# Three elementwise additions of a two-layer graph attention kernel: on GpSimd, or inside accumulating DMAs

## Chip, cores and metric

One core of one Trainium2 chip runs the whole kernel. The metric is the device time of one execution in microseconds (us); less is better. Engines are named as in the profile: PE is TensorE's matmuls and PEld its weight loads, DVE is VectorE, ACT is ScalarE, POOL is GpSimd, SP is SyncE, which issues DMAs here.

## What is computed

The input x has 8 batches of 2048 rows of 256 floats, and one adjacency matrix of 2048 x 2048 serves both layers. All arithmetic is in fp32.

```
# layer 0: attention with 4 heads, a softmax of its own for each chunk of 256 keys
scores = clip(q @ k.T / 8, -10, 10), or -10 where adj == 0
ctx    = sum over the 8 chunks of softmax(scores) @ v
out    = ctx @ Wo.T + bo + x
out    = layernorm(out) * gamma + beta
x      = layernorm(x + out)
# layer 1: graph attention
Wh        = x @ W
e         = leaky_relu(s_i + s_j), -inf where there is no edge
h_prime   = softmax(e) @ Wh
x         = layernorm(x + elu(h_prime))
```

Three of these additions matter here: bo + x ahead of the first layer norm of layer 0, x + beta, which is added back after gamma, and x + elu(...) at the end of layer 1.

## The kernel before

Each batch is worked off in four blocks of 512 queries (`IB`), and each block in 8 chunks `j` of 256 keys, so that there are 8 x 4 x 8 = 256 steps `J`. A step has two halves, called beats; a beat takes about 8 us. The order of all instructions on every engine is written out by hand: a beat issues the scores of 128 keys, their exponentials, the products with v of the step before, and then lets every open generator advance by one `yield`. Each engine executes its own list in order, so an instruction that waits holds up all that stand behind it on its engine.

In layer 0, a beat has the score matmuls of both pairs of heads (L899), the clip and mask on VectorE (L909), the exponential on ScalarE (L912), and the products with v and with ones (L928). The sum of a chunk's weights travels by small DMAs (`dc`, `rd`, `r`, L944 to L956) and comes back as a factor; VectorE multiplies the chunk's product with it (L963, into `un`), and GpSimd adds it to the running context `ctxT` (L964).

Layer 1 of a batch runs beside layer 0 of the next one, at most 1.5 steps of 128 neighbours a beat. A step is a sum on ScalarE (L714), leaky relu (L718) and edge mask (L723) on VectorE, an exponential (L727) on ScalarE, four matmuls (L746, in the last batch L761), and for the row sums an addition on GpSimd into `acc` (L734, L736). Maxima over the edges are made ahead on VectorE (L438), from rows `fb` that DMAs bring. When layer 0 of the last batch is over, layer 1 of the last two batches' blocks remains as a tail.

Two generators hold the changed lines.

- `fin(b, ib, ctxT)` ends a block of layer 0. It is opened three chunks before the block's end. It loads 512 rows of x (L346, by SP), and one beat later GpSimd makes y = x + bo (L349) and x = x + beta (L350), both on 128 x 1024 floats. Once the context is ready, the output projection runs on TensorE (L357), VectorE adds it to y (L364), statistics follow (`stats`, L316 to L322), ScalarE normalizes (L329), GpSimd multiplies with gamma and adds x (L370, L371; in the very last block VectorE does this), and a second layer norm gives the rows of layer 1, which are stored to HBM (`h_d`, L376) and transposed by TensorE (L383).
- `fin1(b, ib, hx, acc)` ends a block of layer 1 in all batches but the last. It loads the block's input rows from `h_d` into `hr` (L591), forms row sums on TensorE (L597), divides on ScalarE (L601), takes the exponential (L603), makes elu on VectorE (L605), has GpSimd add `hr` (L606), and then comes a layer norm and the store (L611). The last batch has a function of its own, `fin1_last`, which adds on VectorE (L632) and is not changed.

The tiles `x`, `y`, `hx` and `hr` have one buffer each: a block's first write to one of them waits until the block before has done with it. The helper `bc_rows(v)` views a row of 256 floats, which lies in all 128 partitions, as four equal rows, so that it fits 128 x 4 x 256.

Of the kernel before, what the change touches and what calls it, by code (L numbers as in the profile page):

```python
# [9 lines left out]
F32 = mybir.dt.float32  # L10
# [4 lines left out]
ALU = mybir.AluOpType  # L15
# [4 lines left out]
P = 128  # L20
# [8 lines left out]
def tile_adj_attention__then__gat(  # L29
# [35 lines left out]
    nc = tc.nc  # L65
    B, N, F = x.shape
# [4 lines left out]
    IB = 512  # L71
    NIB = N // IB
    TPB = IB // P
# [13 lines left out]
    one = ctx.enter_context(tc.tile_pool(name="one", bufs=1))  # L87
# [130 lines left out]
    def row_bc(name, v):  # L218
        t = const.tile([P, F], F32, name=name)
        nc.sync.dma_start(out=t, in_=v.partition_broadcast(P))  # L220
        return t

    bo_bc = row_bc("bo_bc", bo)
    gamma_bc = row_bc("gamma_bc", gamma)
    beta_bc = row_bc("beta_bc", beta)
# [3 lines left out]
    for n in range(2):  # L229
        t = one.tile([P, F], F32, tag=("hx", "ex")[n], name=f"a_bc{n}")  # L230
# [80 lines left out]
    def stats(src, name):  # L311

        st = two.tile([P, TPB, 6], F32, tag="st", name=f"st_{name}")
        mv = two.tile([P, TPB, 2], F32, tag="mv", name=f"mv_{name}")
        for t in range(TPB):
            nc.vector.bn_stats(st[:, t, :], src[:, t, :])  # L316
            nc.vector.bn_aggr(mv[:, t, :], st[:, t, :])
            if t == TPB // 2 - 1 and beat < 2 * NIB * NCH:
                yield
        rstd = two.tile([P, TPB], F32, tag="rstd", name=f"rstd_{name}")  # L320
        nc.vector.tensor_scalar_add(rstd, mv[:, :, 1], EPS)
        nc.gpsimd.tensor_tensor(rstd, rstd, nhalf, ALU.pow)  # L322
        return mv, rstd

    def normalize(dst, mv, rstd, name):
        nmr = two.tile([P, TPB], F32, tag="nmr", name=f"nmr_{name}")
        nc.vector.scalar_tensor_tensor(nmr, mv[:, :, 0], -1.0, rstd, ALU.mult, ALU.mult)
        for t in range(TPB):
            nc.scalar.activation(  # L329
                dst[:, t, :], dst[:, t, :], AF.Identity, bias=nmr[:, t : t + 1], scale=rstd[:, t : t + 1]  # L330
            )

    def bc_rows(v):
        return v.unsqueeze(1).to_broadcast([P, TPB, F])

    h_d = dram.tile([B, NIB, P, TPB, F], F32, name="h_d")
# [5 lines left out]
    def fin(b, ib, ctxT):  # L342


        xt = one.tile([P, TPB, F], F32, tag="x", name=f"x{b}_{ib}")
        nc.sync.dma_start(out=xt, in_=x[b, ts(ib, IB), :].rearrange("(t p) f -> p t f", p=P))  # L346
        yield
        y = one.tile([P, TPB, F], F32, tag="y", name=f"y{b}_{ib}")
        nc.gpsimd.tensor_add(y, xt, bc_rows(bo_bc))  # L349
        nc.gpsimd.tensor_add(xt, xt, bc_rows(beta_bc))  # L350
        while (b, ib) not in ctx_done or ctx_done[b, ib] == beat:
            yield
        for t2 in range(TPB // 2):
            po = ps_m.tile([P, 2, F], F32, tag="m", name=f"po{b}_{ib}_{t2}")
            for j in range(2):
                for k in range(KC):
                    nc.tensor.matmul(  # L357
                        po[:, j, :],
                        ctxT[:, k, ts(2 * t2 + j, P)],
                        WT["o"][:, k, :],  # L360
                        start=(k == 0),
                        stop=(k == KC - 1),
                    )
            nc.vector.tensor_add(y[:, ts(t2, 2), :], po, y[:, ts(t2, 2), :])  # L364
        mv, rstd = yield from stats(y, f"a{b}_{ib}")
        yield
        normalize(y, mv, rstd, f"a{b}_{ib}")
        yield
        engine = nc.vector if (b, ib) == (B - 1, NIB - 1) else nc.gpsimd
        engine.tensor_mul(y, y, bc_rows(gamma_bc))  # L370
        engine.tensor_add(y, y, xt)  # L371
        yield
        mv, rstd = yield from stats(y, f"b{b}_{ib}")
        yield
        normalize(y, mv, rstd, f"b{b}_{ib}")
        nc.sync.dma_start(out=h_d[b, ib], in_=y)  # L376
        fin_near[b] += 1
        yield
        hT = four.tile([P, KC, IB], F32, tag="xT", name=f"hT{b}_{ib}")
        for k in range(KC):  # L380
            pt = ps_m.tile([P, TPB, P], F32, tag="m", name=f"pt{b}_{ib}_{k}")
            for t in range(TPB):
                nc.tensor.transpose(pt[:, t, :], y[:, t, ts(k, P)], ident)  # L383
            nc.scalar.copy(hT[:, k, :], pt.rearrange("p t c -> p (t c)"))
        if (b, ib) == (B - 1, NIB - 1):
            states[b]["hT"] = hT
        else:
            nc.sync.dma_start(out=hT_d[b, ib], in_=hT)
# [198 lines left out]

    def fin1(b, ib, hx, acc):

        hr = one.tile([P, TPB, F], F32, tag="hr", name=f"hr{b}_{ib}")  # L590
        nc.sync.dma_start(out=hr, in_=h_d[b, ib])  # L591
        yield


        pr = ps_m.tile([P, TPB], F32, tag="m", name=f"pr{b}_{ib}")
        for t in range(TPB):
            nc.tensor.matmul(pr[:, t : t + 1], acc[:, ts(t, P)], ones[:, 0:1], start=True, stop=True)  # L597
        r = two.tile([P, TPB], F32, tag="r1", name=f"r1{b}_{ib}")
        nc.vector.reciprocal(r, pr)
        for t in range(TPB):  # L600
            nc.scalar.activation(hx[:, t, :], hx[:, t, :], AF.Identity, bias=ones[:, 0:1], scale=r[:, t : t + 1])  # L601
        ex = one.tile([P, TPB, F], F32, tag="ex", name=f"ex{b}_{ib}")
        nc.scalar.activation(ex, hx, AF.Exp, bias=shifts[:, 1:2])  # L603
        yield
        nc.vector.scalar_tensor_tensor(hx, ex, 1.0, hx, ALU.min, ALU.max)  # L605
        nc.gpsimd.tensor_add(hx, hx, hr)  # L606
        yield
        mv, rstd = yield from stats(hx, f"c{b}_{ib}")
        yield
        normalize(hx, mv, rstd, f"c{b}_{ib}")  # L610
        nc.sync.dma_start(out=out[b, ts(ib, IB), :].rearrange("(t p) f -> p t f", p=P), in_=hx)  # L611
# [92 lines left out]
    class Step:  # L704
# [33 lines left out]
        def product(self):  # L738
# [29 lines left out]
            if last:  # L768
                blocks_done += 1
                tag = "y" if k["b"] == B - 1 and k["ib"] % 2 else "hx"  # L770
                hx = one.tile([P, TPB, F], F32, tag=tag, name=f"hx{self.name}")
                if k["b"] < B - 1:
                    nc.scalar.copy(hx, k["us"])
                else:
                    r = two.tile([P, TPB], F32, tag="r1", name=f"r1{self.name}")
                    for n in range(TPB // 2):
                        nc.vector.reciprocal(r[:, ts(n, 2)], k["us"][n][:, :, F])

                    for t in (0, 2):
                        nc.scalar.activation(  # L780
                            hx[:, t, :],
                            k["us"][t // 2][:, t % 2, 0:F],
                            AF.Identity,
                            bias=ones[:, 0:1],
                            scale=r[:, t : t + 1],
                        )
                        nc.vector.tensor_scalar(
                            hx[:, t + 1, :],
                            k["us"][t // 2][:, t % 2 + 1, 0:F],
                            r[:, t + 1 : t + 2],  # L790
                            1.0,
                            ALU.mult,
                            ALU.add,
                        )
                    fins.append(fin1_last(k["b"], k["ib"], hx))
                    return
                fins.append(fin1(k["b"], k["ib"], hx, k["acc"]))
# [75 lines left out]
    for J in range(total + 1):  # L873
        b, ib, j = J // (NIB * NCH), J // NCH % NIB, J % NCH
# [4 lines left out]
        for half in range(2):  # L879
# [37 lines left out]
            if prev is not None:  # L917
                if half == 0:

                    pool, tag = (one, "hr") if early and J % 3 == 2 else (two, "un")  # L920
                    prev["un"] = pool.tile([P, 2, IB], F32, tag=tag, name=f"un{prev['name']}")
                for part in ((2, 0), (1,))[half]:
# [14 lines left out]
                    else:  # L937
# [7 lines left out]
                            out=dc, in_=ds.rearrange("(h m) (n w) -> h m n w", m=DH, n=DH)[:, 0, :, :]  # L945
# [12 lines left out]
                        def scaled(p=prev):  # L958
                            r2 = p["r"].unsqueeze(1).to_broadcast([P, 2, IB])
                            if p["j"] == 0:  # L960
                                nc.vector.tensor_mul(p["ctxT"], p["un"], r2)
                            else:
                                nc.vector.tensor_mul(p["un"], p["un"], r2)  # L963
                                nc.gpsimd.tensor_add(p["ctxT"], p["ctxT"], p["un"])  # L964
                            if p["j"] == NCH - 1:
                                ctx_done[p["b"], p["ib"]] = beat
                            if p["j"] == NCH - 3:
                                fins.append(fin(p["b"], p["ib"], p["ctxT"]))
# [66 lines left out]
```

## Time and profile before

| | |
|---|---|
| runs | 4401.98, 4400.04, 4389.66 us; median 4400.04 |
| the profiled execution | 4387.29 us, its span 4385.5 us |
| busy in the span | PE 4064.2, DVE 3417.7, ACT 2564.4, POOL 1760.5 us |
| mean granted TensorE clock | 0.98 |
| DMA engines, mean busy share | 30.5% of 16 engines' span, 415.63 MB moved |
| L349, L350, L606 on POOL | 32, 32 and 28 instructions, 2426, 2693 and 2853 ns on average |

A group of instructions is shown as line, engine, operation, what it writes and reads by the program's names, partitions x elements, and how often; then its busy time and the mean duration of one in ns; then the idle time of its engine just before it and what ended most of that idle time. Durations come from the one profiled execution. DMA issues on SP are in the trace as instructions of SP's queue (SPq); they are not counted as busy, and what they move shows only as DMA time.

### The profile page before, as it was taken

The page shows a single profiled execution, that of the slowest core. Times are in us where ns is not written, and L with a number is a line of the kernel's source. Part 1 is how long each engine was busy: PE and PEld are TensorE (multiplying, and loading weights), DVE is VectorE, ACT ScalarE, POOL GpSimd, SP SyncE. Part 2 cuts the span into 40 slices and gives each one's busy share as a digit, 9 for nine tenths or more (in the row PEclk, how much of TensorE's full clock was granted, in tenths as well). Part 3 has the DMA queues.
Part 4 walks back from the last instruction along what each step waited for, and adds up shares of the span by engine and source line. Part 5 has one row for each costly group of instructions (what it writes and reads, how often), then busy time and mean ns, then how long its engine had stood idle before and what let it go on. Part 6 is the DMA issues. An engine that isn't in the chain of part 4 may idle for free. (4 is left out here: it accounts for less than half of the span.)

```text
span 4385.5 us, 61171 instructions
## 1 busy us (share of the span) xinstructions
PE 4064.2 (93%) x23053; PEld 1907.6 (43%) x23053; DVE 3417.7 (78%) x4530; ACT 2564.4 (58%) x3842; POOL 1760.5 (40%) x901
## 2 busy tenths in 40 slices
PE   8889989999999999999899999999999999899767
PEld 3223334454344534454344543445434454344456
DVE  5876589965998669976699766996579965888777
ACT  5655556665566556666566665566556665555546
POOL 0222235543455334444245442554325542354420
PEclk9999999999999999999999999999999999999889
DMA  5554232222332233321333223232232222322321
GB/s 166 182 163 149 71 115 86 83 73 89 99 90 81 64 107 102 100 75 51 105 102 98 74 74 105 85 95 78 70 106 85 89 78 67 115 83 80 123 73 58
DMA packets 257641, 415.63 MB, mean 95 GB/s; under 512 B 85440, under 2 KB 120512, under 8 KB 256448
## 3 DMA queue, kind: packets, MB, share of 16 engines
q1 hardware_dynamic: 257344, 411.71, 30.5%
q8 instruction: 181, 2.97, 0.3%
q14 instruction: 116, 0.95, 0.1%
HBM read 340.66 MB, written 68.88 MB: 93 GB/s over the span
## 5 line engine op out<-in xcount | busy, mean ns | idle before, releaser
L912 ACT ACTIVATE e<-sc 128x1024 f32<-128x1024 f32 x1024 | 1034.2, 1020 | 1049.9 <-DVE sc L909 1006.7
L909 DVE SCALAR_TENSOR_TENSOR sc<-sc,mk 128x1024 f32<-128x1024 f32 x1024 | 1206.7, 1223 | 538.3 <-PE sc L899 352.6
L899 PE MATMUL sc<-qT,kT 64*128 64x512 f32 x4096 | 1060.4, 633 | 86.7 <-ACT e L912 86.2
L964 POOL TENSOR_TENSOR ctxT<-ctxT,un 128x1024 f32<-128x1024 f32 x224 | 568.5, 2538 | 1145.3 <-DVE un L963 1007.0
L928 PE MATMUL u<-e,v 128*32 128x512 f32 x8192 | 980.9, 597 | 0.0
L746 PE MATMUL us<-wh,w 128*128 128x256 f32 x3584 | 878.6, 395 | 81.9 <-ACT w L727 60.4
L746 PEld LDWEIGHTS us<-wh,w 128*128 128x128 f32 x3584 | 667.7, 193 | 422.2 <-ACT w L727 110.7
L736 POOL TENSOR_TENSOR acc<-acc,w 128x512 f32<-128x512 f32 x392 | 601.7, 1535 | 544.9 <-ACT w L727 534.4
L899 PEld LDWEIGHTS sc<-qT,kT 64*128 64x128 f32 x4096 | 347.2, 189 | 611.6 <-ACT e L912 281.8
L718 DVE SCALAR_TENSOR_TENSOR w<-ab,sj,w 128x512 f32<-128x512 f32 x512 | 571.5, 1137 | 4.6 <-ACT w L714 4.5
L928 PEld LDWEIGHTS u<-e,v 128*32 128x32 f32 x8192 | 240.6, 110 | 659.7 <-issue 543.9
L928 PE MATMUL u<-e,ones 128*32 128x512 f32 x4096 | 497.5, 604 | 0.0
L723 DVE TENSOR_TENSOR w<-w,mk 128x512 f32<-128x512 f32 x512 | 458.6, 917 | 37.1 <-DMA mk<-mask 34.6
L438 DVE CUSTOM_DVE_ANT_0 fb<-sj_row,fb 128x1024 bf16<-128x1024 f32 x240 | 387.8, 1626 | 2.3 <-DMA fb<-far 2.3
L714 ACT ACTIVATE w<-ab,sj 128x512 f32<-128x512 f32 x512 | 352.2, 714 | 8.7 <-POOL acc L734 5.4
L727 ACT ACTIVATE w<-w 128x512 f32<-128x512 f32 x512 | 308.8, 629 | 75.9 <-DVE w L723 75.3
L936 ACT COPY un<-u 128x512 f32<-128x512 f32 x512 | 300.5, 587 | 66.5 <-PE u L928 57.6
L963 DVE TENSOR_TENSOR un<-un,r 128x1024 f32<-128x1024 f32 x224 | 278.1, 1242 | 42.2 <-DMA r<-rd 36.7
L928 PEld LDWEIGHTS u<-e,ones 128*32 128x32 f32 x4096 | 107.8, 110 | 356.5 <-issue 305.4
L950 DVE RECIPROCAL dc<-dc 128x16 f32<-128x16 f32 x256 | 63.9, 249 | 149.8 <-DMA dc<-ds 134.0
L942 ACT COPY ds<-u 128x512 f32<-128x512 f32 x256 | 148.5, 580 | 3.0 <-PE u L928 2.5
L349 POOL TENSOR_TENSOR y<-x,bo_bc 128x1024 f32<-128x1024 f32 x32 | 77.6, 2426 | 163.6 <-DMA x<-in_x_dram 103.0
(112 smaller groups left out, 3114.7 us busy)
## 6 DMA issues: line engine op xcount, KB each, us to landing
r<-rd SPq DMA_DIRECT2D x256, 256.0 KB
mk<-mask SPq DMA_DIRECT2D x120, 512.0 KB
fb<-far SPq DMA_DIRECT2D x240, 256.0 KB
xT_k<-in_xT_dram SPq DMA_DIRECT2D x32, 512.0 KB
raw<-in_adjT_dram SPq DMA_DIRECT2D x32, 512.0 KB
rawf<-in_adj_dram SPq DMA_DIRECT2D x32, 512.0 KB
x<-in_x_dram SPq DMA_DIRECT2D x32, 512.0 KB
h_d<-y SPq DMA_DIRECT2D x32, 512.0 KB
```

Source lines behind the costliest of these rows:

```text
L438: nc.vector.tensor_tensor_reduce(out=fb, in0=row, in1=fb, scale=1.0, scalar=2 * FAR * 0.999, op0=ALU.add, op1=ALU.max, accum_out=dst,)
L714: nc.scalar.activation(self.w, k["ab"][:, 1, :], AF.Identity, bias=k["sj"][:, 1, c : c + 1])
L718: nc.vector.scalar_tensor_tensor(self.w, k["ab"][:, 0, :], k["sj"][:, 0, c : c + 1], self.w, ALU.add, ALU.max)
L723: nc.vector.tensor_tensor(self.w, self.w, self.k["mks"][self.c // HT][:, self.c % HT, :], ALU.min)
L727: nc.scalar.activation(self.w, self.w, AF.Exp)
L736: nc.gpsimd.tensor_add(k["acc"], k["acc"], self.w)
L746: nc.tensor.matmul(k["us"][:, t, :], self.w[:, ts(t, P)], k["wh"][c // TPB][:, c % TPB, 0:F], start=(first and t % 2 == 0), stop=last, ski ...
L899: nc.tensor.matmul(sc[:, h, :], kTs[b][c // TPB][h * D : (h + 1) * D, hp, ts(c % TPB, P)], qT[h * D : (h + 1) * D, hp, :], start=True, sto ...
L909: nc.vector.scalar_tensor_tensor(scs[hp], scs[hp], -CLIP, cap, ALU.max, ALU.min)
L912: nc.scalar.activation(e, scs[hp], AF.Exp)
L928: nc.tensor.matmul(m[h * DH : (h + 1) * DH, :], prev["v"][pc // TPB][:, pc % TPB, f0 : f0 + DH] if part < 2 else ones[:, 0:DH], prev["es"] ...
L964: nc.gpsimd.tensor_add(p["ctxT"], p["ctxT"], p["un"])
```

## The change

In `fin`, the tile x is first filled with rows of beta and the tile y with rows of bo, by DMAs from SBUF to SBUF that SP issues. Then two DMAs that GpSimd issues bring the rows of x from HBM and add them to what lies in the tile, first to x and, one beat later, to y. In `fin1`, the tile `hr` and its load go; a DMA that GpSimd issues brings the rows of `h_d` and adds them onto elu's result, and the statistics come one beat later than before.

```diff
     def fin(b, ib, ctxT):
         xt = one.tile([P, TPB, F], F32, tag="x", name=f"x{b}_{ib}")
-        nc.sync.dma_start(out=xt, in_=x[b, ts(ib, IB), :].rearrange("(t p) f -> p t f", p=P))
+        nc.sync.dma_start(out=xt, in_=bc_rows(beta_bc))
         yield
         y = one.tile([P, TPB, F], F32, tag="y", name=f"y{b}_{ib}")
-        nc.gpsimd.tensor_add(y, xt, bc_rows(bo_bc))
-        nc.gpsimd.tensor_add(xt, xt, bc_rows(beta_bc))
+        nc.sync.dma_start(out=y, in_=bc_rows(bo_bc))
+        x_rows = x[b, ts(ib, IB), :].rearrange("(t p) f -> p t f", p=P)
+        nc.gpsimd.dma_start(out=xt, in_=x_rows, accum_op=ALU.add)
+        yield
+        nc.gpsimd.dma_start(out=y, in_=x_rows, accum_op=ALU.add)
         while (b, ib) not in ctx_done or ctx_done[b, ib] == beat:
             yield
...
     def fin1(b, ib, hx, acc):
-        hr = one.tile([P, TPB, F], F32, tag="hr", name=f"hr{b}_{ib}")
-        nc.sync.dma_start(out=hr, in_=h_d[b, ib])
         yield
...
         nc.vector.scalar_tensor_tensor(hx, ex, 1.0, hx, ALU.min, ALU.max)
-        nc.gpsimd.tensor_add(hx, hx, hr)
+        nc.gpsimd.dma_start(out=hx, in_=h_d[b, ib], accum_op=ALU.add)
+        yield
         yield
         mv, rstd = yield from stats(hx, f"c{b}_{ib}")
```

On GpSimd's list 92 DMA issues stand where 92 additions stood; SP's list has 64 issues where it had 60. The wait for beta's rows lies on GpSimd, ahead of the first accumulating DMA, and the wait for the y of the block before lies on SP, ahead of the load of bo's rows. In the changed kernel the two accumulating DMAs of `fin` are lines 352 and 354, which the prediction names so.

## The prediction

> **What bounds the kernel now.** I read the page's busy shares first, then the waits of TensorE, then the groups of GpSimd and VectorE, then the timeline where the changed lines run.
>
> ```profile
> PE 4064.2 (93%) x23053; PEld 1907.6 (43%) x23053; DVE 3417.7 (78%) x4530; ACT 2564.4 (58%) x3842; POOL 1760.5 (40%) x901
> ```
>
> TensorE is the bound: its 4064 us stay as they are. No change off TensorE can be worth more than its idle time, 4385.5 - 4064.2 = 321 us. Its waits (us in total, times, longest):
>
> ```profile
> PE sc L899 <- ACT e L912: 86.2, 57, 6.3
> PE us L746 <- ACT w L727: 60.4, 43, 10.8
> ...
> PE po L357 <- POOL ctxT L964: 16.4, 13, 2.6
> ```
>
> The first two end chains that pass through VectorE (L909 feeds e, L723 feeds w). GpSimd ends only 16.4 us of TensorE's waits, so unloading GpSimd by itself is worth little. The stages (length, then busy us of PE, PEld, DVE, ACT, POOL; granted clock) show one exception to TensorE's rule:
>
> ```profile
> 660.00:3950.00 3290.00, 3125.59 (x17920) 1471.19 (x17912) 2602.62 (x3393) 1959.91 (x2962) 1454.82 (x749) 0.99 0.29 87
> 4110.00:4245.00 135.00, 78.53 (x314) 55.85 (x310) 114.66 (x176) 50.53 (x90) 58.38 (x29) 0.78 0.34 109
> ```
>
> From 4110 to 4245 us VectorE is 85% busy and TensorE 58%: there VectorE sets the pace. Now the three GpSimd groups that go (busy, mean ns):
>
> ```profile
> L350 POOL TENSOR_TENSOR x<-x,beta_bc 128x1024 f32<-128x1024 f32 x32 | 86.2, 2693 | 2.5
> L606 POOL TENSOR_TENSOR hx<-hx,hr 128x1024 f32<-128x1024 f32 x28 | 79.9, 2853 | 43.2 <-DVE hx L605 43.2
> ...
> L349 POOL TENSOR_TENSOR y<-x,bo_bc 128x1024 f32<-128x1024 f32 x32 | 77.6, 2426 | 163.6 <-DMA x<-in_x_dram 103.0 <-PE sc L899 50.4 <-PE pv L275 10.2
> ```
>
> VectorE's two-input operations have long tails (min/median/max ns):
>
> ```profile
> L718 DVE SCALAR_TENSOR_TENSOR w<-ab,sj,w x512: 651/746/2884, 620.5 to 4366.9; 128x512 f32<-128x512 f32 x171
> L723 DVE TENSOR_TENSOR w<-w,mk x512: 674/685/2862, 628.4 to 4367.7; 128x512 f32<-128x512 f32 x171
> ```
>
> The timeline says why. Two L723, 1.4 us by their median, took 4.85 us while L349 and L350 ran:
>
> ```profile
> 2015.15 2.38 POOL L349 TENSOR_TENSOR y<-x,bo_bc 128x1024 f32<-128x1024 f32 x1
> 2017.61 2.69 POOL L350 TENSOR_TENSOR x<-x,beta_bc 128x1024 f32<-128x1024 f32 x1
> ```
>
> ```profile
> 2015.99 4.85 DVE L723 TENSOR_TENSOR w<-w,mk 128x512 f32<-128x512 f32 x2
> ```
>
> **What the Trainium skill says.** (1) "SBUF — State Buffer", section "Who interferes with whom": a VectorE instruction with two SBUF inputs shares a read port with a GpSimd instruction that reads SBUF, and one waits for the other to finish. The trace agrees: 4.85 us against 1.4. (2) "DMA: Bandwidth & Descriptors", "SWDGE vs HWDGE vs iDMA": an accumulating DMA is GpSimd's alone, and its cores write the descriptors; nothing before shows it. (3) Same page, "Anatomy of one DMA — SWDGE (gpsimd) path": about 2.0 us + bytes/436 GB/s, descriptor building "small, variable". (4) "Collectives: The Full Stack", "The bandwidth ceiling": the add costs two source reads in place of one.
>
> **The change, part by part.**
>
> *Removed from GpSimd:* 77.6 + 86.2 + 79.9 = 243.7 us of 1760.5. Off the path, as shown.
>
> *Removed from VectorE: stalls.* Each group's mean on the page, above its fastest instruction: L718 512 x (1137-651) = 249 us, L723 512 x (917-674) = 124, L438 240 x (1626-1186) = 106, small rows some 70; in all about 550. By share of busy GpSimd the removed lines own 244/1760 = 14%, 76 us. By the timeline, giving each instruction's excess to the GpSimd operations that it overlaps, it is L349 25, L350 70, L606 34: 129 us. I take 129; 76 is the low end.
>
> *How much reaches the end.* In 660 to 3950, TensorE idles 0.10 us per 2 us on average. Summed over the 24 pairs L349/L350 there, it idles 23.3 us in the stretch 6 to 16 us after L349 starts, where the average gives 12; over 25 L606, 10.9 us at 4 to 8 us after, where it gives 5. The excess is 17 us; part belongs to other work at that place, so I take 12 (0 to 17). In the tail VectorE leads: L718 at 4124.9 took 2.83 us, L723 at 4127.8 2.71, L438 at 4138.9 3.37, L718 at 4233.8 2.83; above their usual 0.75, 0.69, 1.21, 0.75 that is 8.3 us. At 4131.86 the chain waits for a transfer of fb anyway, so I take 6 (3 to 8). Five pairs before 660: 2 (0 to 4). Sum: 20 us, from 3 to 29.
>
> *Added on SP:* beta rows take the place of x (32 for 32), 32 bo rows come, 28 hr go: 4 issues more x 0.47 us (x's median) = 2 us, at nothing, since SP mostly waits. Behind y's bo rows stand L952 and L956 (rd, r), whose user L963 comes two beats later (a beat is about 8 us). y's rows wait on SP for the previous y's transposes, done 30 us or more earlier in every block: no new wait. If that cover went, SP would hold up every r.
>
> *Added on GpSimd:* 92 DMA issues. The trace has none; the nearest row is SP's 0.47 us, the upper end the whole fixed-plus-transfer time, 2.0 + 0.52 MB/436 GB/s = 3.2 us, doubled for two reads' sake to 6.6. I take 2.0 us: 184 us, so GpSimd gains 60. L352 waits for beta's rows as L349 waited for x (103.0 us, 12 times), with the same size and place on SP; behind it stand L964 and L736.
>
> *Landing.* Time from issue to use: I take 2.0 + 4.4 (two reads: 2.0 + 2 x 1.2) = 6.4 us, from 3.2 to 13. The cover is one extra beat in each place. The tightest are (b,0), where x landed at 1618.5 and L364 wants y at 1636.5 (18 us for 2.0 + L964's 2.4 + 6.4 = 10.8), and (b,3) of layer 1, where L605 ends at 1023.8 and the statistics, one beat later than now, come at about 1034: 10 us for 6.4. Everywhere else it is 16 us or more. So nothing is late at my value. On VectorE's and ScalarE's queues nothing else moves than these statistics and their scaling, one beat back, behind that beat's L909, L963, L718 and L723; TensorE's queue keeps its order. The store of hx slips the same beat, 8 us, of the 41 us or more before the next L773. The DMA engines are 29% busy in the long stage, so the extra 0.5 MB a block finds room.
>
> *Sum.* Against the profiled execution (4387.3, span 4385.5): 4387.3 - 20 = 4367. The median of the runs shown is 12.7 higher: 4400 - 20 = **4380**.
>
> **The rivals.** *A, the forecast:* 4380, own range 4360 to 4387. *B, the stall only moves:* L964 and L736 start earlier and block VectorE instead, or descriptor building holds the same port. For it: L736 and L964 already own 338 of the 550 us. Against: 2.4 us adds back to back are the longest block there is. About 5 us left: 4395. *C, the stall costs more:* if VectorE's lateness also triggers the half-speed stretches of TensorE's clock, 40% of 129 us shows: 4350. *D, the rows land late (slower):* building and landing at 6.6 us each. Then (b,0) needs 13.2 + 2.4 + 6.6 = 22.2 us of 18: 4.2 x 8 = 34 us of VectorE waiting at L364; (b,3) 13.2 of 10.2: 3 x 7 = 21; GpSimd gains 92 x 6.6 - 244 = 363 us of work, which doubles L357's wait for ctxT: 16; the last L606 in the tail, 5. 76 - 20 = +56: 4456. It decides from building plus landing of about 10 us. For it: VectorE is in order, so one late row holds everything. Against: x's plain load takes under 7 us even behind 1 MB of sj_row (1611.9 to 1618.5).
>
> **How the numbers follow.** A 0.55, B 0.18, C 0.07, D 0.20. About 0.3% (13 us) is what a measurement can tell from no change. Faster: A and C, 0.62; within: B, 0.18; slower: D, 0.20. The range must leave out no more than 0.2: from C's 4348 to part of D, 4440.
>
> **What would show it.** Right: L718, L723, L438 means down by 10 to 25%, VectorE busy some 100 us less, L364 and the statistics L316 not waiting for x or h_d rows, TensorE's busy time unchanged. Wrong: VectorE idle until DMA y or hx; GpSimd blocked by its own issues with L357 waiting more for L964; or VectorE means unchanged, with the excess on L736 and L964.

## The result, and the profile after

The changed kernel takes 4444.65 us (median of 5 runs, 4440.60 to 4445.86) against 4399.86 us (5 runs) before: a ratio of 1.0108, with a 95% interval of 1.0098 to 1.0119. It is slower by 45 us, where 20 us of gain were forecast. The profiled execution took 4443.71 us, its span 4441.9 us, 56.4 us more than before's.

The page of the changed kernel, its busy shares and the two large DMA queues (packets, MB, share of 16 engines' span; "software" is GpSimd's queue):

```profile
PE 4082.2 (92%) x23053; PEld 1915.9 (43%) x23053; DVE 3273.9 (74%) x4530; ACT 2568.0 (58%) x3842; POOL 1576.0 (35%) x901
...
q1 hardware_dynamic: 270208, 413.81, 30.3%
q0 software_dynamic: 37824, 48.24, 7.0%
```

Both engines that were to be relieved were: VectorE is busy 144 us less, GpSimd 185. TensorE's idle time grew all the same, from 321 to 360 us, so something else makes it wait. The other 18 of the 56 us are busy time: TensorE's matmuls took 4082.2 us in place of 4064.2, and its mean granted clock was 0.973 in place of 0.980. VectorE's operations did become shorter at their means (L718's 1137 ns to 1107, L723's 917 to 765, L438's 1626 to 1515); the medians had little to lose:

```profile
L721 DVE SCALAR_TENSOR_TENSOR w<-ab,sj,w x512: 651/746/2859, 638.1 to 4423.0; 128x512 f32<-128x512 f32 x171
L726 DVE TENSOR_TENSOR w<-w,mk x512: 673/683/2849, 645.9 to 4423.8; 128x512 f32<-128x512 f32 x171
```

GpSimd's three groups of DMA issues in the place of the additions:

```profile
L352 POOL DMA_DIRECT2D x<-in_x_dram x32 | 43.6, 1363 | 176.8 <-DMA x<-beta_bc 111.9 <-DVE dc L953 47.9 <-DVE sc L912 17.0
L354 POOL DMA_DIRECT2D y<-in_x_dram x32 | 46.1, 1442 | 47.2 <-DMA y<-bo_bc 25.4 <-PE u L931 19.2 <-issue 2.5
L608 POOL DMA_DIRECT2D hx<-h_d x28 | 25.4, 908 | 43.3 <-DVE hx L607 38.5 <-ACT w L730 2.1 <-ACT w L717 1.9
```

They cost 115 us. From issue to landing the medians are 6.3 us (L352), 7.0 (L354) and 5.7 (L608), the longest 13.4; in the first block of batches 1 to 7, L354's took 12.1 to 12.8. Now TensorE's waits after:

```profile
PE sc L902 <- ACT e L915: 79.1, 56, 6.4
PE us L749 <- ACT w L730: 67.8, 45, 8.2
PE po L361 <- POOL ctxT L967: 56.2, 8, 8.5
PE pab L465 <- ACT ds L945: 25.6, 12, 3.2
```

The third line is the find: the output projection waited 16.4 us in 13 waits, the longest 2.6; now it is 56.2 in 8, one in each batch. The name at the end, GpSimd's addition into `ctxT`, is only the last link. VectorE's waits, before and then after, tell what came ahead of it:

```profile
DVE dc L950 <- DMA dc<-ds: 134.0, 98, 4.7
...
DVE fb L438 <- DMA fb<-far: 2.3, 4, 1.0
```

```profile
DVE dc L953 <- DMA dc<-ds: 214.9, 119, 7.6
...
DVE fb L442 <- DMA fb<-far: 51.9, 16, 7.3
...
DVE y L368 <- DMA y<-in_x_dram: 7.8, 1, 7.8
```

Before, VectorE waited for rows `fb` 2.3 us in all; now 51.9. Both lines that grew wait for transfers that the change doesn't touch. For the rows that the accumulating DMAs bring to `y` it waits once, in the last block of the first batch.

The timeline of one place, where the first block of a batch ends, shows the whole chain (start, duration, engine, instruction; in brackets the idle time before it and what ended it):

```profile
1637.76 0.33 SPq L425 DMA_DIRECT2D sj_row<-sj_d  x1
1638.14 0.90 SPq L434 DMA_DIRECT2D fb<-far  x2
1639.14 0.64 SPq L347 DMA_DIRECT2D x<-beta_bc  x1
...
1644.31 0.63 SPq L350 DMA_DIRECT2D y<-bo_bc  x1
...
1646.89 1.35 POOL L352 DMA_DIRECT2D x<-in_x_dram  x1 [15.67 <-DVE dc L953]
...
1649.75 0.92 SPq L140 DMA_DIRECT2D mk<-mask  x1
...
1650.04 1.84 POOL L354 DMA_DIRECT2D y<-in_x_dram  x1
...
1651.75 1.47 SPq L434 DMA_DIRECT2D fb<-far  x2
...
1660.99 1.23 DVE L442 CUSTOM_DVE_ANT_0 fb<-sj_row,fb 128x1024 bf16<-128x1024 f32 x1 [5.84 <-DMA fb<-far]
...
1663.63 1.22 DVE L966 TENSOR_TENSOR un<-un,r 128x1024 f32<-128x1024 f32 x1
...
1665.00 2.33 POOL L967 TENSOR_TENSOR ctxT<-ctxT,un 128x1024 f32<-128x1024 f32 x1 [13.13 <-DVE dc L953]
...
1667.39 2.08 PE L361 MATMUL po<-WT_o,ctxT 128*128 128x256 f32 x4 [8.15 <-POOL ctxT L967]
```

Read it from the bottom. TensorE waited 8.15 us for `ctxT`; GpSimd made it as soon as VectorE's L966 had run; L966 stood on VectorE's list behind L442, which waited 5.84 us for the `fb` rows issued at 1651.75, 9 us before. The line of L361 shows the first four of the projection's 16 matmuls. The same place before:

```profile
1628.35 1.23 DVE L438 CUSTOM_DVE_ANT_0 fb<-sj_row,fb 128x1024 bf16<-128x1024 f32 x1 [0.64 <-DMA fb<-far]
...
1630.65 0.08 DVE L438 DVE_READ_ACCUMULATOR2_ANT m<- 128x1 f32 x1
1630.65 1.22 DVE L963 TENSOR_TENSOR un<-un,r 128x1024 f32<-128x1024 f32 x1
...
1634.41 3.72 PE L357 MATMUL po<-WT_o,ctxT 128*128 128x256 f32 x16 [2.60 <-POOL ctxT L964]
```

The wait costs more than its own length. All 16 matmuls of the projection took 6.45 us after, where they took 3.72 before. The stretch of the projection, before and then after (length, busy us of PE, PEld, DVE, ACT, POOL, granted clock, DMA share, GB/s):

```profile
1634.40:1642.00 7.60, 7.59 (x44) 4.33 (x48) 6.47 (x16) 1.42 (x2) 0.73 (x1) 1.00 0.34 105
```

```profile
1667.40:1675.00 7.60, 7.60 (x22) 5.59 (x24) 3.96 (x8) 1.40 (x2) 0.00 (x0) 0.64 0.34 105
```

The granted clock was 0.64 there in place of 1.00. Batches 1 to 7 all show it: ahead of the first block's projection TensorE waited 0.3 to 2.6 us before and 6.5 to 8.5 after, and the projection took 5.3 to 6.5 us after, against 3.72 before in six of the seven. In sum that is 46 us more of waiting and 13 more of projection.

And why the rows came late. The stretch around those loads, in the same columns, first before, then after:

```profile
1611.00:1619.00 8.00, 8.00 (x54) 2.40 (x56) 3.99 (x5) 3.80 (x5) 0.36 (x1) 1.00 0.75 265
...
1622.00:1630.00 8.00, 7.12 (x50) 1.97 (x52) 7.36 (x9) 3.55 (x6) 5.64 (x2) 1.00 0.57 159
```

```profile
1638.00:1647.00 9.00, 9.00 (x62) 2.66 (x64) 3.97 (x5) 3.80 (x5) 0.11 (x1) 1.00 0.93 285
...
1649.00:1659.00 10.00, 9.70 (x64) 2.56 (x64) 6.15 (x7) 4.51 (x6) 2.88 (x2) 1.00 0.99 216
```

Where the `fb` rows are due, the DMA engines were 57% busy, and are 99% busy now for 10 us. The mean over the long stage, 0.29 before and 0.36 after, shows none of this.

To place the loss, the start of each score matmul (L899, L902) after is set against its start before, in the two profiles. How much each kind of stretch grew (us; one profile each, so that some us are chance):

| stretch | growth |
|---|---|
| batches 1 to 7, first block | -7.1 |
| second block: its first beats, where `fin` of the first block runs | +50.2 (5.1 to 10.0 in each batch) |
| third block | -15.7 |
| fourth block (beats 4 to 6) | +19.3 |
| first batch, with the start | +10.2 |
| tail | -0.5 |

### The profile page after: what moved, and what is told of

The parts are those of the page before. It is cut to its first block, busy times and chain, and to the rows that moved or that the text cites. A ratio compares the mean times of both kernels' runs of the same rounds, so it can differ in the third digit from the quotient of the medians.

```text
span 4441.9 us, 61341 instructions
## 1 busy us (share of the span) xinstructions
PE 4082.2 (92%) x23053; PEld 1915.9 (43%) x23053; DVE 3273.9 (74%) x4530; ACT 2568.0 (58%) x3842; POOL 1576.0 (35%) x901
## 5 line engine op out<-in xcount | busy, mean ns | idle before, releaser
L915 ACT ACTIVATE e<-sc 128x1024 f32<-128x1024 f32 x1024 | 1037.2, 1021 | 1146.6 <-DVE sc L912 1099.9
L912 DVE SCALAR_TENSOR_TENSOR sc<-sc,mk 128x1024 f32<-128x1024 f32 x1024 | 1206.2, 1223 | 549.9 <-PE sc L902 308.7
L902 PE MATMUL sc<-qT,kT 64*128 64x512 f32 x4096 | 1054.9, 629 | 79.7 <-ACT e L915 79.1
L967 POOL TENSOR_TENSOR ctxT<-ctxT,un 128x1024 f32<-128x1024 f32 x224 | 555.7, 2481 | 1251.9 <-DVE un L966 1019.5
L739 POOL TENSOR_TENSOR acc<-acc,w 128x512 f32<-128x512 f32 x392 | 584.9, 1492 | 585.8 <-ACT w L730 575.7
L902 PEld LDWEIGHTS sc<-qT,kT 64*128 64x128 f32 x4096 | 344.7, 188 | 604.1 <-ACT e L915 268.7
L721 DVE SCALAR_TENSOR_TENSOR w<-ab,sj,w 128x512 f32<-128x512 f32 x512 | 556.0, 1107 | 17.3 <-ACT w L717 17.1
L726 DVE TENSOR_TENSOR w<-w,mk 128x512 f32<-128x512 f32 x512 | 380.9, 765 | 38.1 <-DMA mk<-mask 35.5
L442 DVE CUSTOM_DVE_ANT_0 fb<-sj_row,fb 128x1024 bf16<-128x1024 f32 x240 | 361.7, 1515 | 51.9 <-DMA fb<-far 51.9
L966 DVE TENSOR_TENSOR un<-un,r 128x1024 f32<-128x1024 f32 x224 | 272.6, 1217 | 38.0 <-DMA r<-rd 37.8
L361 PE MATMUL po<-WT_o,ctxT 128*128 128x256 f32 x512 | 133.9, 418 | 60.4 <-POOL ctxT L967 56.2
```

Of the source, the lines that this page charges most:

```text
L442: nc.vector.tensor_tensor_reduce(out=fb, in0=row, in1=fb, scale=1.0, scalar=2 * FAR * 0.999, op0=ALU.add, op1=ALU.max, accum_out=dst,)
L721: nc.vector.scalar_tensor_tensor(self.w, k["ab"][:, 0, :], k["sj"][:, 0, c : c + 1], self.w, ALU.add, ALU.max)
L726: nc.vector.tensor_tensor(self.w, self.w, self.k["mks"][self.c // HT][:, self.c % HT, :], ALU.min)
L739: nc.gpsimd.tensor_add(k["acc"], k["acc"], self.w)
L902: nc.tensor.matmul(sc[:, h, :], kTs[b][c // TPB][h * D : (h + 1) * D, hp, ts(c % TPB, P)], qT[h * D : (h + 1) * D, hp, :], start=True, sto ...
L912: nc.vector.scalar_tensor_tensor(scs[hp], scs[hp], -CLIP, cap, ALU.max, ALU.min)
```

## The experiments

The theory after these views, *crowding*: where a batch begins, the two fills and the two accumulating DMAs of `fin` fill the DMA engines just when the `fb` rows are due; VectorE's list waits, then `ctxT`, then TensorE. Rivals: the statistics that `fin1` moves one beat back cost the time; GpSimd's list is held at L354 by the wait for bo's rows; or the fills' place in SyncE's queue, ahead of the `fb` loads, and not the engines' time. The expectations name theories by numbers as they stood when each was written. "Second block" and "fourth block" below are the growth of those rows of the table.

**1. Only the change of `fin1`.** The diff of `fin1` as in the change; `fin` as before.

> Only the part in fin1 is changed: h + elu by an accumulating DMA, statistics one beat later; fin adds on GpSimd as before. Theory 1 (crowded DMA engines in the first block of each batch delay fb's rows and hold VectorE's list, and the moved statistics collide with layer 0's in the fourth block): the collision costs about 20 us, the L606 stalls that are gone give back about 8, so about 4412 us, between 4400 and 4422, with the steps at (b,3) of about 4 us and none at the end of (b,0). Theory 2 (GpSimd's list stands at L354, which waits for bo's rows, ahead of the last addition to ctxT): nothing of the loss is here, about 4390. Theory 3 (accumulated rows land late): VectorE waits at the statistics, some 2 us x 28, about 4450.

Measured: 4387.79 us, 0.9982 (0.9975 to 0.9988). This half is a small gain, against the expectation. Second block +3.4, third -14.8, fourth +24.7: the loss in the fourth block belongs here, the one in the second doesn't.

**2. Only the change of `fin`.** The diff of `fin` as in the change; `fin1` as before.

> Only the part in fin is changed: bo and beta rows filled by SP, x accumulated onto both; fin1 adds hr on GpSimd as before, statistics where they were. Theory 1: the 7 to 8 us at the end of every (b,0) stay, the 4 us in (b,3) go: about 4430 us, between 4420 and 4440. Theory 2: all of the loss is here: about 4445. Theory 3: about 4420, with L368 waiting for y.

Measured: 4449.28, 1.0124 (1.0110 to 1.0137). Second block +46.5, first batch with the start +11.9, third -0.5, fourth -2.0. So the loss is all `fin`'s, nearly all of it at one place of batches 1 to 7, and taking L349 and L350 off GpSimd gained nothing anywhere else. The halves add up: +54 us here and -8 in experiment 1 make 46; the whole change measured 45.

**3. Before, with the second `yield` of `fin1` alone.**

```diff
         nc.gpsimd.tensor_add(hx, hx, hr)
         yield
+        yield
         mv, rstd = yield from stats(hx, f"c{b}_{ib}")
```

> The kernel before with nothing but the second yield behind GpSimd's addition in fin1, so that the statistics of layer 1 come one beat later; no DMA accumulates. Theory 1: the collision in (b,3) alone, about 4 us x 5 to 8: about 4420 us, between 4410 and 4430. Theories 2 and 3: no difference, 4400.

Measured: 4402.00, 1.0014 (1.0007 to 1.0021); fourth block +26.9, first and third -6.5 and -6.7. The moved statistics do cost, but give most of it back elsewhere. Against it, experiment 1, on the same chip and with the same `yield`, is 14 us faster: that is what the accumulating DMA in `fin1` brings, with GpSimd's addition and the load of `hr` gone. In the kernel before, every third `un` also lies in the one buffer of `hr`, and experiment 1 ends that sharing with `fin1` too; which of these parts brings the 14 us was not tried.

**4. After, without that `yield`.**

```diff
         nc.gpsimd.dma_start(out=hx, in_=h_d[b, ib], accum_op=ALU.add)
         yield
-        yield
```

> The changed kernel without its second yield in fin1: the statistics stand where they stood before, one beat after elu, and wait there for the accumulated rows if these are not in. Theory 1: the (b,3) steps go, but with 5.7 us from issue to landing and 0.9 us on GpSimd the rows of the fourth block (3 us between elu and statistics) come 3 to 4 us late, 7 times: about 4430 us, between 4420 and 4440. Theory 2: 4445. Theory 3: slower than the changed kernel, over 4460.

Measured: 4438.19, 1.0094 (1.0079 to 1.0110); second block +49.4, fourth -3.0. The fourth block is mended and the slowdown stays: the rival of the moved statistics falls as the main cause.

The trace shows how the `yield` costs what it does. On VectorE after, in a fourth block, the statistics of `fin1` (st_c) now come directly behind those of `fin` (st_a), and the clip L912 stands behind both:

```profile
1392.15 0.42 DVE L316 BATCH_NORM_STATS2 st_a<-y 128x6 f32<-128x256 f32 x1
...
1394.48 0.42 DVE L316 BATCH_NORM_STATS2 st_c<-hx 128x6 f32<-128x256 f32 x1
...
1398.13 2.36 DVE L912 SCALAR_TENSOR_TENSOR sc<-sc,mk 128x1024 f32<-128x1024 f32 x2
```

Before, st_c ran at 1357.83 and st_a at 1369.01, 11 us apart. TensorE after:

```profile
1402.08 0.27 PE L465 MATMUL pab<-ident,m 128*8 128x128 f32 x1 [3.16 <-ACT ds L945]
1402.57 5.40 PE L256 MATMUL pk<-xT_k,WT_k 128*128 128x512 f32 x8 [0.22 <-ACT un L939]
```

Before, that wait was 0.90 us (at 1377.07), and the same eight matmuls took 3.70 us. After the longer wait they take 5.40, and the granted clock is 0.69 from 1402.5 to 1408, where it was 1.00 before (1379 to 1384).

**5. After, but `fin` the old way in the first block of batches 1 to 7.**

```diff
+        if ib == 0 and b:
... (load of x by SyncE, the two additions by GpSimd, as before)
+        else:
... (fills and accumulating DMAs, as after)
```

> The changed kernel, but in the first block of every batch after the first fin loads x and adds on GpSimd as before (7 of the 32 blocks). Theories 1 and 2: the steps of 5 to 10 us at the end of those blocks go, 46 us in sum; 4444 - 46 = 4398 us, between 4390 and 4406. If the loss were spread over all 32 blocks (theory 3, late rows everywhere), a fifth of it would go: about 4435.

Measured: 4396.87, 1.0002 (0.9993 to 1.0011), as expected; second block +2.8 in place of +50.2; waits for `fb` 10.5 us in place of 51.9. Seven of 32 blocks carry the slowdown. VectorE's waits for `dc` stay at 201.6 us here, so their growth from 134.0 is not what costs the time.

**6. Before, with five plain stores added.** In the first block of batches 1 to 7, SyncE also stores rows of bo to a scratch tensor that nothing reads.

```diff
+        if ib == 0 and b:
+            for n in range(3):
+                z = dram.tile([P, TPB, F], F32, name=f"z{b}_{n}")
+                nc.sync.dma_start(out=z, in_=bc_rows(bo_bc))
         nc.gpsimd.tensor_add(y, xt, bc_rows(bo_bc))
         nc.gpsimd.tensor_add(xt, xt, bc_rows(beta_bc))
+        yield
... (two more such stores, if ib == 0 and b)
```

> The kernel before, all additions on GpSimd, with DMA bytes alone added at the disputed place: in the first block of 7 batches SP issues three stores of bo's rows (512 KB each) one beat after x's load and two more a beat later, to DRAM that nobody reads. Theory 1 (crowded DMA engines): a step of 5 to 9 us at each of the 7 places, about 4440 us, between 4425 and 4455, with VectorE waiting for fb there. Theory 2 (GpSimd's list waits at L354): nothing is added to GpSimd's list, so 4395 to 4400.

Measured: 4423.31, 1.0062 (1.0049 to 1.0075); second block +25.3, waits for `fb` 20.9 us, the output projection's for `ctxT` 31.5. Extra traffic there, which nobody waits for, makes the same waits, but the loss is 27 us where some 40 were expected, just outside the range.

**7. After, with bo's rows loaded one beat earlier.** If GpSimd's list were held at L354 by them, this would free it.

```diff
         nc.sync.dma_start(out=xt, in_=bc_rows(beta_bc))
-        yield
         y = one.tile([P, TPB, F], F32, tag="y", name=f"y{b}_{ib}")
         nc.sync.dma_start(out=y, in_=bc_rows(bo_bc))
+        yield
```

> The changed kernel with bo's rows loaded together with beta's, one beat earlier, so that L354 finds them in place. The bytes are the same. Theory 1: they are only spread a little: about 4440 us, between 4428 and 4450. Theory 2: the wait of GpSimd's list goes and with it the loss: about 4400.

Measured: 4454.30, 1.0132 (1.0118 to 1.0146), second block +58.6, waits for `fb` 59.6. GpSimd's wait ahead of L354 went from 47.2 us to 0, and the loss stayed: the rival of GpSimd's list falls. That it is worse may be because both fills now meet the 1 MB of `sj_row`; no run shows it apart.

**8. The part that pays: `fin` as before, `fin1` with the accumulating DMA, and no second `yield` in the block where the statistics collide.** That is the second block of layer 1, which ends in the fourth block of layer 0.

```diff
-        nc.gpsimd.tensor_add(hx, hx, hr)
+        nc.gpsimd.dma_start(out=hx, in_=h_d[b, ib], accum_op=ALU.add)
         yield
+        if ib != 1:
+            yield
```

> The fin1 part alone, without the second yield in the second block of each batch, whose moved statistics fell together with layer 0's (within 2 us, 6 times); there the rows have about 8 us from elu to the statistics and need 0.9 + 5.7. Theory 1: the seven steps of 4 to 5 us at (b,3) go, some 30 us: about 4362 us, between 4355 and 4375. If the steps have another cause: 4388, as with all second yields.

Measured: 4366.00, 0.9927 (0.9914 to 0.9940), faster than both kernels; first block -10.7, second +0.8, third -18.2, fourth +0.3, tail -5.5.

**9. Before, with that `yield` alone.** GpSimd still adds.

```diff
         nc.gpsimd.tensor_add(hx, hx, hr)
         yield
+        if ib != 1:
+            yield
```

> The kernel before, all additions on GpSimd, with the second yield of fin1 in all blocks but the second of each batch: the moved statistics of the fastest version without its accumulating DMA. It shares that version's gain of 30 us out: by the runs so far the yield alone gave +27 us at (b,3), which should now be gone, and about -15 elsewhere, so about 4382 us, between 4374 and 4390. If the accumulating DMA makes all of the gain: 4396.

Measured: 4375.75, 0.9966 (0.9953 to 0.9979). So about half of experiment 8's 0.73% is re-timing that needs no DMA; the accumulating DMA, with what it removes, is worth the rest, about 0.4%.

**10. After, with `fin` of the first block opened a chunk, two beats, earlier.** The same DMAs, moved to where the engines have room (10% busy two beats earlier in the changed kernel, from 1623 to 1639 us).

```diff
-                            if p["j"] == NCH - 3:
+                            if p["j"] == NCH - (4 if p["ib"] == 0 else 3):
```

> The changed kernel with fin of the first block of each batch opened one chunk (two beats, 16 us) earlier, where the DMA engines are 10% busy and not 88%; the same DMAs, bytes and lists otherwise. Theory 1 (crowded DMA engines): the seven steps go, 4444 - 46 = 4398 us, between 4390 and 4408. If building, waiting or the order on GpSimd's list at the end of the block were the cause, it would stay at 4435 or more.

Measured: 4400.94, 1.0015 (1.0008 to 1.0023), as expected; second block +8.3 in place of +50.2. At the place shown above, in this kernel:

```profile
1645.29 1.23 DVE L442 CUSTOM_DVE_ANT_0 fb<-sj_row,fb 128x1024 bf16<-128x1024 f32 x1 [2.49 <-DMA fb<-far]
1647.58 1.22 DVE L966 TENSOR_TENSOR un<-un,r 128x1024 f32<-128x1024 f32 x1
```

The wait for `fb` is 2.49 us where it was 5.84 (28.0 us in all, where it was 51.9), with every DMA of the change still there. It is their place that costs, not their number.

**11. After, with the fills as ScalarE copies.**

```diff
-        nc.sync.dma_start(out=xt, in_=bc_rows(beta_bc))
+        nc.scalar.copy(xt, bc_rows(beta_bc))
...
-        nc.sync.dma_start(out=y, in_=bc_rows(bo_bc))
+        nc.scalar.copy(y, bc_rows(bo_bc))
```

> The changed kernel with the tiles filled with beta's and bo's rows by two ScalarE copies a block instead of SP's two DMAs; x is still accumulated by GpSimd's DMAs. Theory 1: of the 10.2 us per DMA engine and block (two fills of 1.7, two accumulates of 3.4) a third goes, so about a third of the loss, 15 to 20 us: about 4427 us, between 4412 and 4440. If the accumulates alone are what crowds: 4444. If the fills alone: 4400.

Measured: 4416.74, 1.0052 (1.0039 to 1.0065); second block +28.2. The fills make 22 us of the 50, more than expected.

**12. Before, with one store and two accumulating DMAs added at the same places**, onto scratch tensors in HBM that nothing reads.

```diff
...
+        if dosed:   # ib == 0 and b
+            z = dram.tile([P, TPB, F], F32, name=f"z{b}")
+            nc.sync.dma_start(out=z, in_=bc_rows(bo_bc))
+            nc.gpsimd.dma_start(out=zs[0], in_=x_rows, accum_op=ALU.add)
         nc.gpsimd.tensor_add(y, xt, bc_rows(bo_bc))
         nc.gpsimd.tensor_add(xt, xt, bc_rows(beta_bc))
+        yield
+        if dosed:
+            nc.gpsimd.dma_start(out=zs[1], in_=x_rows, accum_op=ALU.add)
```

> The kernel before, all additions on GpSimd, with the real mix of DMAs added in the first block of 7 batches: one store of bo's rows by SP and two accumulating DMAs of x's rows by GpSimd, all onto DRAM that nobody reads; its wait for rows on GpSimd is left out. Plain stores of the same engine time gave 27 us of the 46. If a queue of its own lets the accumulates push SP's fb loads further back: about 4440 us, between 4432 and 4450. If the missing 19 us come from GpSimd's list in the changed kernel: 4423 again.

Measured: 4425.53, 1.0081 (1.0067 to 1.0096); second block +34.8, but waits for `fb` of only 6.6 us in all. Less than the 4432 to 4450 expected, and by another chain than in the changed kernel. GpSimd's list has the additions and the issues here, so this run is no clean dose.

**13. After, with the fills in ScalarE's queue.** The same bytes, but no longer in one list with the `fb` loads.

```diff
-        nc.sync.dma_start(out=xt, in_=bc_rows(beta_bc))
+        nc.scalar.dma_start(out=xt, in_=bc_rows(beta_bc))
...
-        nc.sync.dma_start(out=y, in_=bc_rows(bo_bc))
+        nc.scalar.dma_start(out=y, in_=bc_rows(bo_bc))
```

> The changed kernel with the two fills issued on ScalarE's queue in place of SyncE's: the same bytes at the same place, but no longer in one list with the fb loads. If the fb rows are late because the fills stand ahead of them in SyncE's queue, the loss at the first blocks falls from 50 to about 28 us, as it did with fills by copies: about 4420. If they are late because the DMA engines have too much to move, whatever the queue, it stays near 50: 4440 to 4450, with 45 us or more of waits for fb. I expect the second, 4442.

Measured: 4463.39, 1.0151 (1.0135 to 1.0167), second block +56.8, waits for `fb` 40.6, for `dc` 232.9. Another queue frees nothing: the rival of the place in SyncE's queue falls as the main cause. The place is not quite the same, since ScalarE issues beta's fill some 6 us earlier against TensorE's work. That another queue doesn't help, the Trainium skill says too ("DMA: Bandwidth & Descriptors", "Issuing engines are not separate DMA queues": whatever engine starts them, DMAs run on the same 16 engines). It is 19 us slower than the changed kernel, of which the second block shows 7; ScalarE's exponential L915 waits 4.7 us for a fill's turn. The rest wasn't followed up.

**14. After, with plain DMAs in place of the accumulating ones in those seven blocks.** These blocks then lack bo and beta.

```diff
+        acc_kw = {} if ib == 0 and b else {"accum_op": ALU.add}
-        nc.gpsimd.dma_start(out=xt, in_=x_rows, accum_op=ALU.add)
+        nc.gpsimd.dma_start(out=xt, in_=x_rows, **acc_kw)
...
```

> The changed kernel, but in the first block of each batch from the second on the two DMAs of GpSimd are plain, without the addition (bo and beta are left out of these blocks): half the DMA engine time for the same issues at the same places. If engine time is what delays the fb rows, 2 x 1.7 us an engine fewer at each place, the loss there falls from 50 to about 35: about 4430. If only the issue on GpSimd or the number of packets counts, it stays at 50: 4444. I expect 4430.

Measured: 4429.51, 1.0076 (1.0061 to 1.0091), as expected; second block +33.8. The number of the issues, their bytes and their places are the same; the DMA engines' time is less. The packets of each are fewer as well (128 of 4 KB in place of 512 of 1 KB), and GpSimd's issues there are shorter (0.84 and 0.79 us in place of 1.35 and 1.84). Their length is hardly a rival: at the place shown GpSimd idled 13.13 us between L354 and the last addition to `ctxT`. GpSimd's queue in this kernel:

```profile
q0 software_dynamic: 32448, 48.24, 6.5%
```

**15. The same, with the fills of those blocks left out too.**

```diff
+        if ib or not b:
             nc.sync.dma_start(out=xt, in_=bc_rows(beta_bc))
...
```

> As the kernel before this one, and in the same blocks the two fills are left out too (bo and beta are left out of these blocks): what remains of the change there are two plain 512 KB loads issued by GpSimd in place of one issued by SyncE. If the bytes in the crowded stretch are the cause, 0.5 MB more than before is left of 2 MB of engine time, and the loss falls to some 12 us: about 4405. If GpSimd's issues, with their waits ahead of ctxT's additions, are the cause, it stays above 30: about 4425. I expect 4405.

Measured: 4411.93, 1.0034 (1.0020 to 1.0049); second block +16.5, where 12 was expected. Against experiment 14 nothing differs but the fills, and with them GpSimd's waits for their rows; they are worth 17 us. From L354's issue to its landing it takes 12.6 us at these places in the changed kernel, 8.4 in experiment 14 and 4.5 here, on average.

**What they give together.** A transfer's price is the DMA engines' time. GpSimd's queue took 7.0% of 4441.9 us, over 92 DMAs 3.38 us an engine for each 512 KB; experiment 14 took 6.5% of 4425.9, and with 78 DMAs still at 3.38 the 14 plain ones come to 1.7. The fills in a queue of their own (experiment 13: 2.4% of 4453.3 over 64) come to 1.67. An accumulating DMA costs about two plain ones, and not for its packets: the accumulating L608 alone (experiment 1: 2.0% of 4392.0 over 28, in packets of 4 KB) comes to 3.1, L352 and L354 alone (experiment 2: 5.1% of 4448.2 over 64, 1 KB) to 3.5, and the fills move in packets of 1 KB too. Before, `fin` moved 1.7 us an engine here; set against that:

| kernel | extra time of each DMA engine there, us | growth of the second block, 7 batches |
|---|---|---|
| 5: old way | 0 | 2.8 |
| 15: two plain loads | 1.7 | 16.5 |
| 11: accumulating, fills by ScalarE | 5.1 | 28.2 |
| 14: fills, plain loads | 5.1 | 33.8 |
| the change; 13: fills in another queue | 8.5 | 50.2; 56.8 |
| 10: the change, two beats earlier | 8.5 elsewhere | 8.3 |

The loss follows the engines' time, about 6 us for each us (7 batches x 0.8 to 0.9), whichever of the transfers is taken away. The added traffic of 6 and 12, some 10 us an engine, cost 25 and 35, below this line; their transfers are other ones, to HBM, and what chain made 12 slow stays open, as does the loss of 10 us in the first batch: it is `fin`'s (11.9 in 2, 0.8 in 1), and no run was made to take it further apart.

## Why the prediction was wrong

*TensorE's 4064 us "stay as they are".* Wrong by 18 us: the projections of the first blocks took 13 us more behind their longer waits, and the matmuls L256 for k 13 more, some 10 of them in the fourth blocks, where the moved statistics collide; the scores took 5 less.

*GpSimd's additions, off the path.* Right: 243.7 us of additions went. It was busy 185 us less, with 115 of issues in their place and the other additions shorter, and no gain came from that by itself.

*VectorE's stalls.* Right in size: I took 129 us of excess for GpSimd's three lines. Measured the same way, the excess over the fast instructions fell by some 149 us, from about 550 to about 400, and the new issues own some 20. What the Trainium skill says in "SBUF — State Buffer", "Who interferes with whom", held: the stalls went with the additions that read SBUF, and only a small part came back with the issues. Rival B is refuted by that: L736's part fell by some 35 us, L964's rose by 9.

*How much reaches the end, 20 us.* Wrong in its parts. The pairs L349 and L350, from which most of my 12 us in the long stage came, gave nothing (experiment 2). So what I read as TensorE's idle time behind them was other work's, or was filled by other waits; which, no run shows. L606, credited with a small part of those 12 and of the 6 in the tail, gave 14 us with its load (1 against 3). In the tail the whole change gained 0.5 us of 6. Rival C's gain did not come. The link that it took, from lateness to slow stretches of TensorE's clock, did show, but on the side of the loss: the granted clock of 0.64 behind the 8.15 us wait.

*SyncE's queue, "at nothing".* The fills cost SyncE as little as said: 0.64 us each where x's load took 0.5. But they, not SyncE's time, were the expense, 22 us of the 50 (experiment 11).

*GpSimd's issues, 2.0 us each.* Too high: 1.25 on average. (The upper end, 3.2 doubled, is 6.4 and not 6.6; little hangs on it.) *Landing, 6.4 us:* right at the medians, 5.7 to 7.0, but twice that for L354 in the seven first blocks. *"So nothing is late":* nearly right for the rows themselves: VectorE waited once for `y`, 7.8 us in the last block of the first batch, where the cover was not the 16 us or more of "everywhere else", and 0.6 for `hx`. Rival D, the slower case, named 4456, near the 4444.65 measured, by luck: its chain is wrong, since not the accumulated rows were late, but those of others.

**The step that failed** is the last sentence of the part on landing: "The DMA engines are 29% busy in the long stage, so the extra 0.5 MB a block finds room." It fails three times. It counted bytes added, 0.5 MB, where the engines' time goes up by 8.5 us each, five times what the one load took: the fills count too, and an accumulating DMA counts twice, which I had used for the landing and not for the load. It took a mean over 3290 us for a place at which `sj_row` (1 MB), the mask and four `fb` loads meet, and where 57% was already taken. And "Behind y's bo rows stand L952 and L956" looked only at SyncE's list for the next few entries, and not at the `fb` loads 7 us further, whose user L438 stands ahead of L963 on VectorE. What the runs showed in its place: the DMA engines 99% busy for 10 us, `fb` rows late by up to 7.3 us (51.9 in all), and 50 us lost at the projections of seven blocks. Undoing the change at that place alone removes the slowdown (5); moving the same DMAs two beats earlier removes 42 of 50 us (10); halving the engine time of those DMAs removes 16 (14).

*Statistics one beat back, at nothing.* Wrong as well. That they come "behind that beat's L909, L963, L718 and L723" is what I checked; what I didn't was that in one block of four they meet `fin`'s own statistics. It costs 19 to 27 us in the fourth blocks, and the same `yield` gains in others: +0.14% net (3). Leaving it out in that block is worth 22 us (8 against 1).

*The end:* 4367 was the sum for the profiled execution; it took 4443.71. The kernel lost 50 us in the second blocks, 19 in the fourth and 10 in the first batch, where I had expected a gain of 2; that is about the 77 us between the two. The gains in the first and third blocks, 23 us, are about the size of the forecast 20, but by chance: they come from `fin1` and re-timing, not from L349 and L350.

## What to carry to other kernels

Price a DMA that replaces an engine's work by the DMA engines' time at its own place, fills and double cost of accumulation included, and read the DMA share of that stretch, some 10 us long, not of the stage. Then ask whose rows are already due there, and who stands behind their user on an engine that works in order: a late transfer of a third party holds up all of them. A change of two halves is worth splitting before it is judged; here one half, less one `yield`, was the fastest kernel of all.

## What the runs showed of the hardware

- An accumulating DMA of 512 KB took 3.4 us of each of 16 engines, a plain one about 1.7. That fits the two reads in place of one of which the Trainium skill speaks in "Collectives: The Full Stack", "The bandwidth ceiling"; that the second read is what costs, no run shows.
- GpSimd's issue of one took 0.91 us for L608 and 1.36 to 1.44 us for L352 and L354 on average, of the same 512 KB. L608 reads a block that lies whole for each partition and moves in 128 packets of 4 KB; L352 and L354 read four rows of 1 KB for each partition and move in 512 packets of 1 KB. The plain form of the latter (14 of their 64 issues in experiment 14) moves in 128 packets of 4 KB as well, and took 0.84 and 0.79 us to issue: the time went with the packets, not with the accumulation.
- GpSimd's 92 issues beside two-input VectorE work cost that work some 20 us, where the 92 additions had cost some 130.
- After TensorE had waited 6.5 to 8.5 us, the 16 matmuls of a projection took 5.3 to 6.5 us; after waits of at most 2.6 us they took 3.72 in six of seven cases. The granted clock was 0.64 in the stretch shown of the first kind and 1.00 in that of the second.
